# Last feed-forward of a transformer block: one activation per rounding, wider places for the output projections, x added by TensorE for half the tiles

## The chip, the cores and the metric

The kernel runs on 1 core of one Trainium2 chip. The metric is the device time of the whole program in microseconds (us). The core has five engines that matter here, each with its own in-order queue: PE (TensorE: matmuls, and transposes as matmuls with an identity), DVE (VectorE), ACT (ScalarE), POOL (GpSimd) and SP, which here issues the DMAs. They wait for one another through semaphores.

## The reference, cut to what matters

x has 2 sequences of 2048 tokens with 256 features. The block is: layer norm, attention with 16 heads, residual, layer norm, a gated feed-forward of width 704 whose operands are rounded to 4-bit floats in blocks of 16, residual.

```python
def fp4_quant_dequant(x):
    shape = x.shape
    xb = x.reshape(shape[:-1] + (shape[-1] // BLOCK, BLOCK))
    scale = jnp.max(jnp.abs(xb), axis=-1, keepdims=True) / 6.0
    scale = jnp.maximum(scale, jnp.float32(1e-12))
    xn = xb / scale
    idx = jnp.searchsorted(_MID, jnp.abs(xn))
    q = _GRID[idx] * jnp.sign(xn) * scale
    return q.reshape(shape)

def _L0_ffn_ref(x, w_gate, w_up, w_down):
    gate = fp4_linear(x, w_gate)
    y = fp4_linear(x, w_up)
    h = jax.nn.silu(gate) * y
    return fp4_linear(h, w_down)

h = _layernorm(x, axis=-1) * (1 + ca) + sa
x = x + ga * _L0_attn_ref(h, ...)
h = _layernorm(x, axis=-1) * (1 + cb) + sb
x = x + gb * _L0_ffn_ref(h, ...)
```

`fp4_linear` rounds both operands and multiplies them. sa to gb are vectors of 256 for each sequence.

## The kernel before, in words

A sequence is cut into 16 tiles of 128 tokens. The two sequences run one after the other through attention, head by head; the feed-forward of the first sequence is spread under the attention of the second. The feed-forward of the second has nothing to lie under: it is the last stage, from about 1797 us to the end, and the change touches this stage alone.

No order is written out by hand. Each piece of work is a Python generator (a chain) that yields operations. A planner, `Order`, takes the chains with a due time each, keeps an estimated clock for every engine, and emits the operation that can start earliest by its own cost estimates, preferring the chain due first within a small patience. What it emits is the order in each engine's queue. `Best` lets it choose between two engines, with a margin by which the second has to be better. Places in PSUM are handed out by name: three places "s" of two banks each, and two places "o" of one bank. `Wait` takes a place, `give` returns it. All operations are recorded by one helper, so nearly all of them carry line 253 in the profile, and tiles are told apart by their names.

In the last stage, with b = 1 and q = 3 (the last group of heads):

- `project_last` multiplies the attention output of a tile (`osb`) by the output weights (`wo`, two products of 256 columns into `op`) and adds the result to the tile of `x` on DVE. Tiles 0 and 1 have an "s" place each, of which one bank is used; then two tiles share one bank, those of 6 and 7 in an "s" place and the others in "o" places.
- `ffn_stats` computes the layer norm's statistics (`stf`, `mvf`, `ln0f` to `ln2f`) for tile 0, tiles 1 to 3, and then four tiles at a time.
- `tail_norm` applies them into `w` (one tile for 0 and 1, then two tiles of 256 side by side, 512 wide) and rounds `w` with `quantize`.
- `tail` transposes a rounded tile (`hq`, in an "o" place), copies it to SBUF, multiplies by the gate and up weights (`pg`, `pu`, an "s" place each, four products of 352 columns each), applies silu on ACT, multiplies on DVE into `e` (704 wide), rounds `e` with `quantize`, transposes it (`h2t`, an "s" place), copies it, and multiplies by the down weights `wdb` into `dn`, on top of a product of the identity with `x` that carries the residual. `tail_out` copies `dn` to `y` and stores it. For the last tile `tail_part` does this in two halves of 352.
- `quantize(a, nb, name, m, margin)` rounds in place: maximum of each block (`am`), reciprocal and scale (`r`, `s`, `q`), multiplication by `r`, the exponents of the result into `m` by a bit mask, from these a magic constant for each element, addition and subtraction of it (which rounds), and multiplication by `s`. In the last stage `margin` is a number, elsewhere it is None. For the constants the planner chooses between two passes on ACT and one on DVE. In the last stage DVE does the addition, POOL or DVE the subtraction and the last multiplication.

The due times of the last stage are relative to d, the end of the attention steps:

```python
add(
    project_last(b, NQUAD - 1, t, 1 if t < 2 else 2),
    d + PROJECT_DUE[t // 4] + (0.1 * t if t < 4 else 0.0),
)
```

Of the kernel before, what the change touches and what calls it, by code (L numbers as in the profile page):

```python
# [10 lines left out]
F32 = mybir.dt.float32  # L11
# [3 lines left out]
AF = mybir.ActivationFunctionType  # L15
ALU = mybir.AluOpType
# [4 lines left out]
P = 128  # L21
# [18 lines left out]
QUANTIZE_MARGIN = 2  # L40
WEIGHTS_MARGIN = 3
TAIL_MARGIN = 0.5
MAGIC_MARGIN = 2.0


PROJECT_DUE = -0.5, 0.0, 0.2, 0.4
NORM_DUE = -0.4, -0.2, 0.6
STATS_LEAD = 4
NORM_LEAD = 3.5
# [50 lines left out]
class Order:  # L100
# [17 lines left out]
    def add(self, gen, due, pace=0.0):  # L118

        heapq.heappush(self.later, (due, next(self.seq), gen, pace))  # L120


    def signal(self, key, of=1, early=0.0):

        n, t = self.counts.get(key, (0, 0.0))
        n, t = n + 1, max(t, self.chain.end - early)
        self.counts[key] = (n, t)
        if n == of:
            self.done[key] = t
        return n == of  # L130

    def give(self, name, n=1, place=0):
        for _ in range(n):
            heapq.heappush(self.rooms[name], (self.chain.end, place))
# [180 lines left out]
def adaln_block(  # L315
# [15 lines left out]
    B, N, D = x_in.shape  # L331
# [10 lines left out]
    NQUAD = H // 4  # L342
# [12 lines left out]
    T, V, A, G, S = (  # L355
        Queue(n, e)
        for n, e in (
            ("PE", nc.tensor),
            ("DVE", nc.vector),
            ("ACT", nc.scalar),  # L360
            ("POOL", nc.gpsimd),
            ("SP", nc.sync),
        )
# [9 lines left out]
    signal, give, due = order.signal, order.give, order.due  # L373
# [14 lines left out]
    def banks(place, name):  # L388

        return ps_s.tile([P, 2, 512], F32, tag=f"s{place}", name=name)  # L390
# [7 lines left out]
    def either(first, second, margin):  # L398
        return Best(first, second, margin=COPY_MARGIN if margin is None else margin)

    def copy(dst, src, margin=None):
        return either(A.copy(dst, src), V.tensor_copy(dst, src), margin)

    def matmuls(dst, pairs, first=True):
        return [
            T.matmul(dst, lhsT=l, rhs=r, start=(first and k == 0), stop=(k == len(pairs) - 1))
            for k, (l, r) in enumerate(pairs)
        ]
# [22 lines left out]
    def x_tile(b, t):  # L431
        return xs[b, t // 4][:, t % 4, :]
# [153 lines left out]
    def pool(*args, margin):  # L586
        if margin is None:
            return V.tensor_tensor(*args)
        return Best(G.tensor_tensor(*args), V.tensor_tensor(*args), margin=margin)
# [9 lines left out]
    SIXTH = 1.0 / 6.0  # L599

    EXPONENT = 0x7F800000

    SMALLEST = 5.999999976025183e-12

# [3 lines left out]
    def spread(s):  # L608
        return s[:, :].unsqueeze(2).to_broadcast([s.shape[0], s.shape[1], BLK])
# [17 lines left out]
    def quantize(a, nb, name, m, margin=None):  # L627

        a3 = blocks(a)
        yield Wait(take=["qs"])
        am = small.tile([P, nb], F32, tag="am", name=f"am_{name}", bufs=3)
        s = small.tile([P, nb], F32, tag="qs", name=f"s_{name}", bufs=3)
        r = small.tile([P, nb], F32, tag="qr", name=f"r_{name}", bufs=3)
        q = small.tile([P, nb], F32, tag="qq", name=f"q_{name}", bufs=2)  # L640
        yield V.tensor_reduce(am, a3, AX.X, ALU.max, apply_absolute_value=True)
        yield V.tensor_scalar(am, am, SMALLEST, None, ALU.max)
        yield V.reciprocal(r, am)

        yield Free(V.tensor_scalar(s, am, SIXTH, None, ALU.mult))
        yield V.tensor_scalar(r, r, 6.0 - 3 * 2.0 ** -21, None, ALU.mult)
        yield V.scalar_tensor_tensor(q, s, -4.0, am, ALU.mult, ALU.add)
        yield pool(a3, a3, spread(r), ALU.mult, margin=QUANTIZE_MARGIN if margin is None else None)
        yield Free(V.scalar_tensor_tensor(q, s, -2.0, q, ALU.mult, ALU.add))
        yield V.tensor_scalar(m.bitcast(U32), a.bitcast(U32), EXPONENT, None, ALU.bitwise_and)  # L650
        yield Free(V.scalar_tensor_tensor(s, q, SIXTH, s, ALU.mult, ALU.add))
        yield either(

            [
                A.activation(m, m, AF.Relu, bias=magic[:, 1:2], scale=1.5 * 2.0 ** 22),
                A.activation(m, m, AF.Identity, bias=magic[:, 0:1]),
            ],
            V.tensor_scalar(m, m, 1.0, 1.5 * 2.0 ** 22, ALU.max, ALU.mult),
            margin if margin is None else MAGIC_MARGIN,
        )  # L660
        yield pool(a, a, m, ALU.add, margin=QUANTIZE_MARGIN if margin is None else None)
        for args in ((a, a, m, ALU.subtract), (a3, a3, spread(s), ALU.mult)):
            op = G.tensor_tensor(*args)
            yield op if margin is None else Best(op, V.tensor_tensor(*args), margin=margin)
        give("qs")

    def quantize_exactly(x, i, u, name):
# [470 lines left out]
    def project_last(b, q, t, n):  # L1138

        g = t // 4  # L1140
        room = "s" if t in (0, 1, 6) else "o"
        (place,) = yield Wait(
            [("osb", b, q, g), ("wo", b, q), ("x", b, g)]
            + [("out", b, q - 1, t + j) for j in range(n)],
            [room],
        )
        name = f"op{b}_{q}_{t}"
        if room == "s":
            ps = banks(place, name)[:, 0, :]
        else:  # L1150
            ps = ps_o.tile([P, 512], F32, tag="o", name=name)
        for j in range(n):
            yield Free(
                matmuls(
                    ps[:, j * D : (j + 1) * D],
                    [
                        (o_sb[b, 2 * q + k][:, (t + j) * P : (t + j + 1) * P], wos[b, q][:, k, :])
                        for k in range(2)
                    ],
                )  # L1160
            )
        x2 = xs[b, g][:, t % 4 : t % 4 + n, :]
        yield V.tensor_tensor(x2, ps[:, 0 : n * D].rearrange("p (j d) -> p j d", d=D), x2, ALU.add)
        give(room, place=place)
        for j in range(n):
            signal(("out", b, q, t + j))

# [98 lines left out]
    def silu_table():  # L1266
        yield Wait([("w", len(steps) - 1, 0)])
        yield A.activation(sig[:, :, 0], sig[:, :, 0], AF.Silu)
# [185 lines left out]
    for b in range(B):  # L1454
        s0 = b * PER
        if b > 0:
            spread_over([norm(b, g) for g in range(NG)], s0 - 62, s0 - 36, NPACE)
            spread_over([qk(b, 0, i, n) for n in range(NCH) for i in range(2)], s0 - 36, s0 - 14)
            spread_over([qk(b, 1, i, n) for n in range(NCH) for i in range(2)], s0 + 16, s0 + 6 * NT)
            spread_over([load_x(b, g) for g in range(NG)], s0 + 2 * NT, s0 + 3 * NT)  # L1460
        for q in range(NQUAD):
            e0 = s0 + 4 * q * NT
            if (b, q) != (0, 0):
                add(load_wv(b, q), e0 - 2 * NT)
                spread_over([values(b, q, g) for g in range(NG)], e0 - NT + 3, e0 + 3)
            add(load_wo(b, q), e0 + 2 * NT)
            if (b, q) == (B - 1, NQUAD - 1):
                continue
            o0 = e0 + 4 * NT + 2
            spread_over(  # L1470
                [project(b, q, g) for g in range(NG)], o0, o0 + (20 if q == NQUAD - 1 else 40)
            )
        if b < B - 1:
            f0 = s0 + PER + 10
            for t in range(NT):
                if t % 4 == 0:
                    add(ffn_stats(b, t, 4), f0 + FFN * t - 1)
                add(ffn(b, t), f0 + FFN * t, FPACE)
        else:
            d = s0 + PER + LAG - 1  # L1480
            add(weight_tail(), s0 + PER - 6)
            add(silu_table(), d - 0.2)
            for t in (0, 1, *range(2, NT, 2)):
                add(
                    project_last(b, NQUAD - 1, t, 1 if t < 2 else 2),
                    d + PROJECT_DUE[t // 4] + (0.1 * t if t < 4 else 0.0),
                )
                if t < 4:
                    dues = d + NORM_DUE[(t + 1) // 2]
                else:  # L1490
                    dues = d + t - STATS_LEAD
                if t == lns_of(t):
                    add(ffn_stats(b, t, (1, 3)[t] if t < 4 else 4), dues)
                add(tail_norm(b, t, 1 if t < 2 else 2), dues if t < 4 else d + t - NORM_LEAD)
            for t in range(NT):
                add(tail(b, t), d + t - (LAST_LEAD if t >= NT - SPLIT else 0))
# [48 lines left out]
```

## Time and profile before

| what | us |
|---|---|
| median of 3 runs | 1987.07 |
| lowest, highest | 1986.43, 1989.49 |
| profiled execution | 1986.46 |
| its span, first to last instruction | 1984.7 |
| PE busy in the span | 1919.7 (97%) |
| DVE busy | 1714.8 (86%) |
| ACT busy | 1341.3 (68%) |
| POOL busy | 622.0 (31%) |
| granted clock of PE, mean | 0.996 |

The page gives busy time, not the bound: a matmul's end is modelled, and a queue that waits for a semaphore is not busy. In the last stage several engines hand each other tiles in turn. Between 1860 and 1880 us, for instance, PE is busy 18.75 of 20 us and DVE 19.32. By form, the last stage's rounding has these rows on ACT and DVE:

| row | count | mean ns |
|---|---|---|
| ACT, constants, 128x704 | 30 | 882 |
| ACT, constants, 128x512 | 14 | 721 |
| DVE, addition or subtraction of them, 128x704 | 29 | 900 |
| DVE, the same, 128x512 | 14 | 675 |
| DVE, multiplication by s, 128x704 | 12 | 879 |
| DVE, x plus projection, 128x512 | 7 | 686 |
| DVE, copy of `h2t`, 118x768 | 2 | 956 |

In a timeline row the first number is the start, the second the time from the first start to the last end of the merged instructions, and the bracket at the end the idle time of the engine before them and what ended it. Every fp32 product is two matmul instructions, which is why four products are listed as x8.

### The profile page before, as it was taken

To read this page: it belongs to the slowest core of one execution; us is meant where nothing else is said; L and a number is where in the kernel's file an instruction comes from. 1 tells how busy PE (TensorE), PEld (TensorE's weight loads), DVE (VectorE), ACT (ScalarE), POOL (GpSimd) and SP (SyncE) were. 2 spreads that over 40 slices of the span, in tenths; PEclk is the share of its full clock that TensorE was granted. 3 is DMA by queue.
4 is the path that set the end of the run, shared out by engine and by line. 5 is a ranking of instruction groups with operands and counts; after the bars stand their busy time and mean duration, and the time that the engine had idled before them with its cause. 6 is when DMAs were issued, how large, how long until landed. Compare 5 with 4: busy or idle time off the path is not lost. (4 is left out here: it accounts for less than half of the span.)

```text
span 1984.7 us, 30266 instructions
## 1 busy us (share of the span) xinstructions
PE 1919.7 (97%) x10196; PEld 782.1 (39%) x10196; DVE 1714.8 (86%) x4125; ACT 1341.3 (68%) x1438; POOL 622.0 (31%) x1387
## 2 busy tenths in 40 slices
PE   8999999999999989999999999999999999998988
PEld 5323333233333333343333444334343333325666
DVE  5999889988999998879888688897788878998897
ACT  3677767777777676776777667685676767783444
POOL 0233333333343331112444344444443111230100
PEclk9999999999999999999999999999999999999999
DMA  6322121112111123211011201211011111100000
GB/s 212 84 61 59 37 59 49 38 33 49 33 45 33 38 64 91 75 38 49 14 46 56 63 24 38 54 36 38 4 36 43 33 33 33 33 1 0 13 12 19
DMA packets 40395, 88.02 MB, mean 44 GB/s; under 512 B 6320, under 2 KB 22576, under 8 KB 36272
## 3 DMA queue, kind: packets, MB, share of 16 engines
q1 hardware_dynamic: 38880, 83.98, 16.4%
q10 hardware_dynamic: 1360, 2.10, 0.3%
q8 instruction: 82, 1.34, 0.3%
q14 instruction: 73, 0.60, 0.1%
HBM read 63.51 MB, written 20.97 MB: 43 GB/s over the span
## 5 line engine op out<-in xcount | busy, mean ns | idle before, releaser
L253 DVE TENSOR_SCALAR_CACHE_REDUCE e<-ps 128x1024 f32<-128x1024 f32 x1024 | 1221.7, 1218 | 141.1 <-PE ps L253 92.3
L253 ACT ACTIVATE e<-e,mn 128x2048 f32<-128x2048 f32 x512 | 1025.4, 2003 | 435.2 <-POOL mn L253 432.2
L253 PE MATMUL o<-e,vn 128*64 128x512 f32 x4096 | 995.5, 604 | 24.3 <-POOL vn L253 18.8
L253 PEld LDWEIGHTS o<-e,vn 128*64 128x64 f32 x4096 | 253.4, 136 | 482.8 <-issue 350.9
L253 POOL TENSOR_SCALAR mn<-mn 128x1 f32<-128x1 f32 x512 | 154.6, 302 | 832.9 <-DVE rz L253 344.4
L253 PE MATMUL ps<-q,k 64*128 64x512 f32 x2048 | 383.5, 448 | 5.4 <-DVE e L253 2.1
L253 PEld LDWEIGHTS ps<-q,k 64*128 64x128 f32 x2048 | 157.3, 185 | 377.9 <-DVE rz L253 109.2
L253 POOL TENSOR_SCALAR vn<-v,rz 128x64 f32<-128x64 f32 x512 | 169.4, 331 | 305.9 <-DVE rz L253 233.4
L253 PE MATMUL op<-wo,osb 128*64 128x256 f32 (+1 forms) x960 | 123.6, 382 | 2.8 <-DVE x L253 2.1
L253 PE MATMUL v<-wv,ht 128*64 128x256 f32 x1024 | 123.3, 383 | 0.6 <-DVE st L253 0.6
L253 DVE RECIPROCAL rz<-z 128x1 f32<-128x1 f32 x512 | 80.3, 157 | 27.0 <-ACT e L253 25.8
L253 PEld LDWEIGHTS op<-wo,osb 128*64 128x64 f32 (+1 forms) x960 | 76.4, 140 | 60.4 <-issue 30.7
L253 ACT ACTIVATION_READ_ACCUMULATOR e<-e,mn 128x1 f32 x512 | 95.4, 186 | 0.0
L253 PEld LDWEIGHTS v<-wv,ht 128*64 128x64 f32 x1024 | 70.5, 137 | 58.6 <-issue 25.6
L253 DVE DVE_READ_ACCUMULATOR e<-ps 128x1 f32 x1024 | 84.7, 83 | 0.0
L253 ACT COPY osb<-o 64x512 f32<-64x512 f32 x101 | 58.4, 579 | 18.6 <-PE o L253 17.2
L253 PE MATMUL qk<-ht,wqk_sb 128*64 128x512 f32 (+1 forms) x224 | 65.8, 605 | 1.3 <-ACT ht L253 0.9
L253 POOL TENSOR_TENSOR h<-h,m 128x704 f32<-128x704 f32 x32 | 54.1, 1690 | 10.3 <-DVE m L253 5.6
L253 DVE TENSOR_TENSOR x<-op,x 128x1024 f32<-128x1024 f32 (+2 forms) x37 | 39.7, 1074 | 15.9 <-PE op L253 15.6
L253 PE MATMUL pg<-wg_t,w 128*128 128x352 f32 x128 | 46.7, 507 | 6.4 <-ACT w L253 6.4
L253 PE MATMUL dn<-wdb,e 117*128 117x256 f32 (+1 forms) x192 | 45.3, 384 | 3.3 <-ACT e L253 2.5
L253 ACT ACT_TABLE_LOAD x34 | 43.6, 1283 | 4.3 <-issue 3.7
(242 smaller groups left out, 1468.8 us busy)
## 6 DMA issues: line engine op xcount, KB each, us to landing
k<-scr SPq DMA_DIRECT2D x124, 256.0 KB, 4.7
scr<-st SPq DMA_DIRECT2D x32, 512.0 KB, 3.1
q<-scr SPq DMA_DIRECT2D x124, 128.0 KB, 5.6
x<-in_x_dram SPq DMA_DIRECT2D x8, 512.0 KB, 4.9
wv<-in_wv_dram SPq DMA_DIRECT2D x8, 256.0 KB, 5.4
wo<-in_wo_dram SPq DMA_DIRECT2D x8, 256.0 KB, 4.2
xt<-in_x_dram SPq DMA_DIRECT2D x4, 512.0 KB, 5.4
out_dram<-h2t SPq DMA_DIRECT2D x16, 128.0 KB, 1.7
```

Source lines behind the costliest of these rows:

```text
L253: op = Op(self.name, *self.estimate(method, args, kw, lambda: f(*args, **kw)))
```

## The change

It has two parts, both in the last stage.

Rounding, where `margin` is a number: ACT makes the constant without its offset in one pass, Relu(MAGIC * m - MAGIC). DVE adds the offset while it adds the constant, and again while it takes the sum away, in two operations with three inputs (tile, number, tile). The second leaves the value negated, and the scale s is negated to match. The subtraction stays on DVE; the last multiplication may still go to POOL. If the planner chooses DVE for the constants, that is two operations now.

Projections: tiles 0 to 3, 4 to 7 and 8 to 11 share one "s" place of two banks each; 12 and 13, and 14 and 15, an "o" place. The additions to `x` are their own chains, `projected`: two of one tile and then of two tiles. For tiles 8 to 15 (`ADD_X = 2` groups of four and above) PE adds x by a product with the identity, and the sum is copied to `x` by ACT or DVE, whichever the planner finds better.

```diff
 PROJECT_DUE = -0.5, 0.0, 0.2, 0.4
+PROJECTED = (0, 4), (4, 4), (8, 4), (12, 2), (14, 2)
+ADD_X = 2
...
+    MAGIC = 1.5 * 2.0 ** 22
...
         yield V.tensor_scalar(m.bitcast(U32), a.bitcast(U32), EXPONENT, None, ALU.bitwise_and)
-        yield Free(V.scalar_tensor_tensor(s, q, SIXTH, s, ALU.mult, ALU.add))
-        yield either(
-
-            [
-                A.activation(m, m, AF.Relu, bias=magic[:, 1:2], scale=1.5 * 2.0 ** 22),
-                A.activation(m, m, AF.Identity, bias=magic[:, 0:1]),
-            ],
-            V.tensor_scalar(m, m, 1.0, 1.5 * 2.0 ** 22, ALU.max, ALU.mult),
-            margin if margin is None else MAGIC_MARGIN,
-        )
-        yield pool(a, a, m, ALU.add, margin=QUANTIZE_MARGIN if margin is None else None)
-        for args in ((a, a, m, ALU.subtract), (a3, a3, spread(s), ALU.mult)):
-            op = G.tensor_tensor(*args)
-            yield op if margin is None else Best(op, V.tensor_tensor(*args), margin=margin)
+        if margin is None:
...
+        else:
+
+            yield Free(V.scalar_tensor_tensor(s, q, -SIXTH, s, ALU.mult, ALU.subtract))
+            yield either(
+                A.activation(m, m, AF.Relu, bias=magic[:, 1:2], scale=MAGIC),
+                [
+                    V.tensor_scalar(m, m, 1.0, MAGIC, ALU.max, ALU.mult),
+                    V.tensor_scalar(m, m, -MAGIC, None, ALU.add),
+                ],
+                MAGIC_MARGIN,
+            )
+            yield V.scalar_tensor_tensor(a, m, MAGIC, a, ALU.add, ALU.add)
+            yield V.scalar_tensor_tensor(a, m, MAGIC, a, ALU.add, ALU.subtract)
+            op = G.tensor_tensor(a3, a3, spread(s), ALU.mult)
+            yield Best(op, V.tensor_tensor(a3, a3, spread(s), ALU.mult), margin=margin)
         give("qs")
...
-        room = "s" if t in (0, 1, 6) else "o"
+        room = "s" if n > 2 else "o"
...
         if room == "s":
-            ps = banks(place, name)[:, 0, :]
+            ps = banks(place, name)
         else:
-            ps = ps_o.tile([P, 512], F32, tag="o", name=name)
...
-        x2 = xs[b, g][:, t % 4 : t % 4 + n, :]
-        yield V.tensor_tensor(x2, ps[:, 0 : n * D].rearrange("p (j d) -> p j d", d=D), x2, ALU.add)
-        give(room, place=place)
+            ps = ps_o.tile([P, 512], F32, tag="o", name=name).unsqueeze(1)
+        taken = [1, 1, 2] if t == 0 else [2] * (n // 2)
+        for k, m in enumerate(taken):
+            first = sum(taken[:k])
+            part = ps[:, first // 2, first % 2 * D : (first % 2 + m) * D]
+            for j in range(m):
+                u = t + first + j
+                pairs = [
+                    (o_sb[b, 2 * q + c][:, u * P : (u + 1) * P], wos[b, q][:, c, :])
+                    for c in range(2)
+                ]
+                if g >= ADD_X:
+                    pairs = [(ident, x_tile(b, u))] + pairs
+                yield Free(matmuls(part[:, j * D : (j + 1) * D], pairs))
+            order.add(
+                projected(b, q, t + first, m, part, order.chain.end, (room, place, t, len(taken))),
+                order.chain.due,
+            )
+
+    def projected(b, q, t, n, ps, ready, where):
+
+        room, place, first, parts = where
+        order.chain.base = ready + order.CROSS
+        x2 = xs[b, t // 4][:, t % 4 : t % 4 + n, :]
+        ps = ps.rearrange("p (j d) -> p j d", d=D)
+        if t // 4 >= ADD_X:
+            yield copy(x2, ps, TAIL_MARGIN)
+        else:
+            yield V.tensor_tensor(x2, ps, x2, ALU.add)
+        if signal(("projected", b, q, first), of=parts):
+            give(room, place=place)
         for j in range(n):
             signal(("out", b, q, t + j))
...
             add(silu_table(), d - 0.2)
+            for t, n in PROJECTED:
+                add(project_last(b, NQUAD - 1, t, n), d + PROJECT_DUE[t // 4])
             for t in (0, 1, *range(2, NT, 2)):
-                add(
-                    project_last(b, NQUAD - 1, t, 1 if t < 2 else 2),
-                    d + PROJECT_DUE[t // 4] + (0.1 * t if t < 4 else 0.0),
-                )
                 if t < 4:
```

## The prediction, made before the changed kernel had run

> **What bounds the kernel now.** I read the windows first, then TensorE's timeline over the last stage, then DVE's waits, then the rows by form. Attention up to 1796 us is untouched: the changed program issues the same instructions in the same order on every engine there. So everything is decided in the last feed-forward, 1797 to 1984.7 us. The windows (busy us of PE, PEld, DVE, ACT, POOL, then granted clock, DMA):
>
> ```profile
> core 0: us, PE busy (x) PEld busy (x) DVE busy (x) ACT busy (x) POOL busy (x), PEclk, DMA share, GB/s
> 1800.00:1820.00 20.00, 12.26 (x50) 9.30 (x49) 19.80 (x98) 2.81 (x7) 0.00 (x0) 0.87 0.00 0
> ...
> 1840.00:1860.00 20.00, 17.63 (x71) 12.38 (x70) 15.59 (x44) 7.88 (x12) 1.38 (x2) 0.91 0.02 7
> ...
> 1880.00:1900.00 20.00, 19.30 (x79) 13.74 (x78) 18.11 (x58) 9.32 (x15) 1.07 (x1) 1.00 0.06 20
> 1900.00:1920.00 20.00, 18.52 (x79) 13.14 (x79) 19.52 (x55) 9.36 (x15) 1.06 (x1) 1.00 0.04 14
> 1920.00:1940.00 20.00, 16.44 (x71) 12.03 (x70) 17.75 (x49) 8.83 (x15) 1.64 (x1) 0.91 0.04 14
> ```
>
> First DVE is full and PE waits; later both are nearly full, and ACT is never half busy. Where PE waits (start, us, form, count, then the wait before it):
>
> ```profile
> 1796.98 10.63 PE L253 MATMUL op<-wo,osb 128*128 128x256 f32 x48
> 1809.70 1.99 PE L253 MATMUL op<-wo,osb 128*128 128x256 f32 x8 [2.09 <-DVE x L253]
> 1816.88 0.69 PE L253 MATMUL hq<-ident,w 128*128 128x128 f32 x2 [5.19 <-DVE x L253]
> 1818.03 4.40 PE L253 MATMUL pg<-wg_t,w 128*128 128x352 f32 x8 [0.46 <-ACT w L253]
> 1822.27 2.53 PE L253 MATMUL pu<-wu_t,w 128*128 128x352 f32 x8
> 1824.64 1.89 PE L253 MATMUL op<-wo,osb 128*128 128x256 f32 x8
> ...
> 1848.77 4.33 PE L253 MATMUL pg<-wg_t,w 128*128 128x352 f32 x8 [1.51 <-ACT w L253]
> ...
> 1869.68 2.63 PE L253 MATMUL pg<-wg_t,w 128*128 128x352 f32 x8 [0.79 <-ACT w L253]
> ...
> 1928.63 0.84 PE L253 MATMUL h2t<-ident,e 128*118 128x128 f32 x6 [3.04 <-DVE e L253]
> ...
> 1950.92 1.45 PE L253 MATMUL pg<-wg_t,w 128*128 128x352 f32 x4 [1.05 <-ACT w L253]
> ```
>
> The first transposes (`hq_0`) wait for DVE's `x` addition and not for the normed tile: w_0 was finished at 1811.0, but both "o" places still held projections. After that wait, and again at 1848.77, the gate product takes 4.4 instead of 2.6: granted clock 0.87 and 0.91. DVE has one long wait of its own, because a copy of transposed data stands in its queue:
>
> ```profile
> 1856.16 0.96 DVE L253 COPY e<-h2t 118x768 f32<-118x768 f32 x1 [3.54 <-PE h2t L253]
> ```
>
> **The change, step by step.** Starts are read from the timeline; pitches are differences of starts: 0.2165 us per matmul instruction of 256 columns (two to a product), so 0.87 for a tile's projection; gate or up product 2.37; DVE 0.34/0.60/0.80 for two-input work 256/512/704 wide.
>
> *Start.* Tiles 8 to 15 get one product each for x: 8 x 0.43 = 3.5 us more PE. In the changed program's queues the waits go by whole places: the addition of tile 0 waits for tile 1's product, tile 2's product for that addition, tile 3's for the next, tile 7's for the addition of 4 and 5, tile 11's for ACT's copy of 8 and 9. From 1797.05: tile 1 ends 1798.8, the first addition starts 1799.0 (now 1798.15), tiles 2, 3, 7 and 11 are held 0.7, 0.6, 0.85 and 0.85 us. PE: 16 x 0.87 + 3.5 + 3.0 held + 0.2 for hq_0 = 20.6, so pg_0 starts about 1817.7 (now 1818.03). DVE reaches w_0 at 1813.4, which is 2.4 later than now: additions start 0.9 later and then wait for products (1.7 more), one w_1 operation of 0.4 moves ahead, and one addition of 0.6 is gone. That is covered: hq_0 stands behind tile 14 and starts at 1816.2. Without the cover it would cost those 2.4.
>
> *Clock and last projection.* PE's longest idle is now 0.9, so pg_0 runs at 2.37 rather than 4.24 to the next start (1.87), and the two projections after pu_0 (1.73) are already done. hq_1 starts 1822.4 against 1826.37: 0.3 + 1.9 + 1.7 = 4.0 gained. DVE has w_1 ready by 1820.7, having four additions fewer; ACT's four copies of 512 (nearest row: 0.586, a 512-wide PSUM copy) lie in its idle time, but the last of them, released at 1817.7, is ahead of w_1's constants; that holds DVE about 0.3.
>
> *Rounding.* ACT loses one pass per quantization: 0.88 at 704 (15 times), 0.72 at 512 (7), about 0.5 at 256 and 352 (4). DVE's two plain additions become two three-input ones. No 704-wide row of these without pointer exists. The nearest: qx_wd 128x352 at 517 ns against 517 for a plain one, qx_wg 128x256 at 418 against 412; so no cost. Upper end: those with pointers at 256, 476 against 410, 0.055 x 52 (two in each of 26 roundings) = 2.9 us. Lower end 0. POOL takes four multiplications by s_g instead of three and a subtraction, no change; SP's queue is identical. All DVE pitches summed: 158.1 us now, 153.5 after: four additions (2.4) and three copies go to ACT (2.2).
>
> *Tiles 0 to 5.* DVE's times here are the pitches summed in the changed order from 1799.0, plus its waits: 1.8 for products, 0.9 where small dependent operations start 0.19 apart and nothing fills in, 0.3 for ACT, then 0.6 for pu_0, together 3.6; PE's are its products in a row. hq_2 needs w_2 from POOL, ready 1827 before pu_1 ends at 1827.9; h2t_0, free at 1837.1, has its e_0 and the place it takes at 1835.8. dn_0 ends 1842.0 (now 1846.2). Then w_4: DVE 1799.0 + 38.8 + 3.6 = 1841.4, POOL 1.06 to 1.64 behind it, so hq_4 at 1843.0 and, one ACT pass less in its queue, pg_4 at 1843.9: a gap of 1.9 for 2.6 now. With the clock kept (1.8), pu_4 ends at 1848.6 against 1855.3: 4.2 + 0.7 + 1.8 = 6.7. Such gaps, from the last product to the next with transposes between, were 2.3 before 1950.92, warm (x4 in 1.45), and 2.6 before 1848.77, cold. 1.9 is below both, so I take warm; cold costs 1.8. The Trainium skill, "TensorE: Matmul & The Clock Gate" (What's actually happening), says the clock falls after an idle window of about 3.4 us, and Part 4 there that transposes do not count as busy. By the window 1.9 stays warm, the trace's 2.6 should have too and did not; by Part 4 the total could fall to 6.7 us.
>
> *Onward.* COPY e_1 goes to ACT and its 3.54 wait with it; h2t_1 comes 6.7 earlier. dn_1, dn_2 hold 0.5 each for ACT copies; pg_6 starts 1862.6 (now 1869.68): 7.1. DVE ends w_6's rounding at 1799.0 + 54.4 + 3.6 = 1857.0 (now 1865.05), so it isn't what PE waits for at hq_6. From there work is alike on both (DVE 99.1 after, 99.4 now; same PE work), so I keep the gap. Added: the wait at 1928.63, whose chain runs through ACT pairs, shortens by one pass, 0.9; the last tile loses a pass of 0.5 on the chain that ends last. Sum: 7.1 + 0.9 + 0.5 = 8.5.
>
> The Trainium skill, "PSUM — Partial Sum Buffer" (PSUM bank collisions raise a hardware error), forbids two engines only in one bank at once; by it tile 2, in the second bank, need not wait, which would give about 0.7 back. The program waits by place, so the trace should show the holds.
>
> The profiled execution took 1986.46, span 1984.7; the median of the three unprofiled runs is 1987.07, 0.6 above, and I carry that over: 1987.07 - 8.5 = **1978.6 us**.
>
> **Rivals.** (A) *More*: the 3.04 wait at 1928 and its cold restart (pg x4 2.52 for 1.35, and slow dn, together 1.9) go entirely: 4.0 on top, 1974.6. For: ACT's queue there holds two pairs, 1.80 and 1.48, halved. Against: two tiles cost DVE about 18.9 of the present 19.1 cadence, so lateness may reappear elsewhere. 0.17.
> (B) *Given back*: DVE is the bound; only its removed work counts, less its later start: 4.6 - 2.4 = 2.2, 1984.9. For: 19.52 of 20 busy in 1900 to 1920. Against: 15.59 in 1840 to 1860, which is PE's lateness. 0.15.
> (C) *Slower*: ACT becomes DVE's gate. Constants and copies share one in-order queue; each copy that waits for PE holds a rounding behind it, and DVE's queue with it. DVE now waits 4.0 us for this in 26 roundings (3.6 and 0.4 by the rows of e), 0.15 each; were each as long as the single wait of 0.64 at 1869, it is 26 x 0.49 = 12.7 more, 1991.3. It decides from 8.5/26 = 0.33 more each. Against: ACT 9.4 of 20 busy, and a pass fewer. 0.08.
> That the change does nothing is excluded: in the queues each constants pass stands once, x is copied by ACT.
>
> **Numbers.** Forecast 0.60, A 0.17, B 0.15, C 0.08. A measurement of this kernel tells about 0.2% (4 us) from no change: faster 0.60 + 0.17 = 0.77, same 0.15, slower 0.08. Range: A and another 1.1 down, 1973.5; up the cold pg_4 (1.8), dearer rounding (2.9) and the unshortened wait (0.9), with 0.3 towards B: 1984.5.
>
> **What would show it.** hq_0 at 1816 with no wait on `x`; pg_0 at 2.4 to 2.6; four short holds among the projections; pg_4 near 1844 and warm; no h2t copy on DVE; three-input rounding rows at 0.88. I am wrong if PE falls to the low clock among the projections, if DVE's waits for ACT exceed 12 us, or if pg_6 is early and the end is not.

## The result, and the profile after

The changed kernel took 1976.99 us (median of 4 runs, 1974.49 to 1977.45) against 1987.43 for the kernel before (4 runs): a ratio of 0.9944, 95% interval 0.9926 to 0.9961. So it is faster by 10.4 us.

The profiled execution of the changed kernel has a span of 1975.7 against 1984.7, 9.0 less. But it entered the last stage late: attention's last product ended at 1799.34 us, and at 1797.05 in the execution of before. The instructions up to there are the same, but TensorE's granted clock was 0.50 for three stretches of 3.41 us in this execution (from 22, 49 and 616 us) and for one in that of before (from 47 us). Over the fourteen profiled executions of this study the stage is entered between 1796.1 and 1799.8. Every edit here touches only what comes after it, so from here on kernels are compared by their **stage**: from the end of attention's last product to the end of the span. It was 187.65 us before and is 176.36 now: 11.3 less. (The expectations below count from the first projection product: 0.07 earlier, but in runs 4 and 12 0.44 later, because there it waits for ACT.)

The windows of the changed kernel, with the columns as before (busy us of PE, PEld, DVE, ACT, POOL, then the granted clock, DMA):

```profile
core 0: us, PE busy (x) PEld busy (x) DVE busy (x) ACT busy (x) POOL busy (x), PEclk, DMA share, GB/s
1800.00:1820.00 20.00, 17.51 (x79) 14.12 (x78) 16.54 (x82) 5.04 (x9) 0.00 (x0) 1.00 0.00 0
...
1840.00:1860.00 20.00, 18.15 (x84) 13.45 (x83) 19.79 (x56) 7.22 (x12) 1.21 (x1) 1.00 0.04 13
...
1920.00:1940.00 20.00, 17.76 (x75) 12.41 (x74) 19.42 (x49) 7.41 (x12) 3.80 (x3) 1.00 0.06 20
```

The clock is 1.00 in all three, where before it was 0.87, 0.91 and 0.91. DVE, which had 15.59 of 20 us to do in 1840 to 1860, is nearly full there.

TensorE's timeline of the changed kernel, at the places shown of before (start, us, form, count, and the wait before it):

```profile
1801.78 1.13 PE L255 MATMUL op<-wo,osb 128*128 128x256 f32 x4 [0.52 <-DVE x L255]
1803.43 3.72 PE L255 MATMUL op<-wo,osb 128*128 128x256 f32 x16 [0.52 <-DVE x L255]
1807.93 1.13 PE L255 MATMUL op<-wo,osb 128*128 128x256 f32 x4 [0.78 <-DVE x L255]
...
1813.62 0.70 PE L255 MATMUL op<-x,ident 128*128 128x256 f32 x2 [0.68 <-ACT x L255]
...
1818.91 0.38 PE L255 MATMUL hq<-ident,w 128*128 128x128 f32 x2
...
1820.42 2.53 PE L255 MATMUL pg<-wg_t,w 128*128 128x352 f32 x8
...
1846.70 2.63 PE L255 MATMUL pg<-wg_t,w 128*128 128x352 f32 x8 [0.44 <-ACT w L255]
...
1866.08 2.63 PE L255 MATMUL pg<-wg_t,w 128*128 128x352 f32 x8 [0.29 <-ACT w L255]
...
1925.95 0.66 PE L255 MATMUL hq<-ident,w 128*128 128x128 f32 x4 [0.94 <-POOL w L255]
1926.90 2.63 PE L255 MATMUL pg<-wg_t,w 128*128 128x352 f32 x8 [0.30 <-ACT w L255]
```

The four holds among the projections are there, the wait of 5.19 for `x` is gone, and no gate product runs at the low clock. The longest wait in the whole stage is the 0.94 near 1926, for POOL; near 1928 before had one of 3.04, for DVE.

The stage can be taken apart on TensorE: products at full clock, with the 3.2 us that follow the last of them, plus idle time, plus what the low clock adds. Idle time is the sum of the waits in the timeline. The changed kernel has hardly a slow product, and 176.36 - 11.50 idle = 164.86; without the eight products with x (0.433 each) it is 161.4. What another kernel has beyond that is put down to the clock (runs 4 and 8 below, whose clock did not fall before the last product, come out at -0.2 and 0.5, which shows how exact this is):

| kernel | stage | idle of PE | clock | median of runs |
|---|---|---|---|---|
| before | 187.65 | 20.7 | 5.6 | 1987.43 |
| changed | 176.36 | 11.5 | 0 | 1976.99 |

So 9.2 us of idle time and 5.6 of slow clock went, and 3.5 of products came in.

By form, DVE's two three-input operations and ACT's one pass (count, then busy us and mean ns of one, then the idle time before):

```profile
L255 DVE SCALAR_TENSOR_TENSOR e<-e 128x704 f32<-128x704 f32 x30 | 26.4, 880 | 1.9 <-ACT e L255 1.9
...
L255 ACT ACTIVATE e<-e,magic 128x704 f32<-128x704 f32 x15 | 13.2, 881 | 8.6 <-DVE e L255 8.6
```

880 ns against 900 for the plain additions and subtractions before, and at 512 wide 686 against 675: the third input costs nothing to speak of.

### The profile page after: what moved, and what is told of

It is laid out like the page before. It is cut to its first block, busy times and chain, and to the rows that moved or that the text cites. A ratio compares the mean times of both kernels' runs of the same rounds, so it can differ in the third digit from the quotient of the medians.

```text
span 1975.7 us, 30282 instructions
## 1 busy us (share of the span) xinstructions
PE 1920.0 (97%) x10212; PEld 783.1 (40%) x10212; DVE 1711.3 (87%) x4118; ACT 1325.7 (67%) x1419; POOL 621.0 (31%) x1387
## 5 line engine op out<-in xcount | busy, mean ns | idle before, releaser
L255 DVE RECIPROCAL rz<-z 128x1 f32<-128x1 f32 x512 | 80.4, 157 | 27.0 <-ACT e L255 25.8
L255 ACT COPY osb<-o 64x512 f32<-64x512 f32 x101 | 58.4, 579 | 18.6 <-PE o L255 17.2
L255 PE MATMUL dn<-wd_t,h2t 117*64 117x256 f32 (+1 forms) x384 | 46.2, 383 | 0.2 <-DVE h2t L255 0.2
```

The source lines that it names most:

```text
L255: op = Op(self.name, *self.estimate(method, args, kw, lambda: f(*args, **kw)))
```

## The experiments

Twelve kernels, all with the same attention. The table has their stage, TensorE's idle time and the clock's share as above, and the median of the whole runs. The kernel before, run beside them, had medians of 1987.43, 1988.42 and 1987.24 in the three groups (1 to 4, 5 to 8, 9 to 12).

| run | stage | idle | clock | median | ratio to before, 95% interval |
|---|---|---|---|---|---|
| 1 rounding only | 176.79 | 13.8 | 1.6 | 1976.95 | 0.9951, 0.9934 to 0.9968 |
| 2 projections only | 188.26 | 18.8 | 4.6 | 1987.13 | 0.9999, 0.9990 to 1.0009 |
| 3 x added on DVE | 187.90 | 22.1 | 4.4 | 1987.53 | 1.0004, 0.9994 to 1.0013 |
| 4 first tiles apart | 175.56 | 10.9 | -0.2 | 1975.49 | 0.9944, 0.9929 to 0.9959 |
| 5 two passes | 179.51 | 12.3 | 2.4 | 1978.68 | 0.9955, 0.9940 to 0.9970 |
| 6 two passes, unplanned | 184.67 | 15.9 | 3.9 | 1984.93 | 0.9980, 0.9971 to 0.9990 |
| 7 one pass, planned two | 178.55 | 11.4 | 2.3 | 1978.12 | 0.9953, 0.9938 to 0.9968 |
| 8 scale on POOL | 175.56 | 10.2 | 0.5 | 1974.60 | 0.9935, 0.9919 to 0.9952 |
| 9 two passes, old order | 187.91 | 18.6 | 4.4 | 1987.28 | 1.0001, 0.9992 to 1.0010 |
| 10 one pass, old order | 188.03 | 18.0 | 5.2 | 1987.93 | 1.0005, 0.9996 to 1.0014 |
| 11 before's order, one pass | 182.32 | 18.8 | 2.1 | 1983.46 | 0.9984, 0.9975 to 0.9993 |
| 12 apart and POOL | 174.76 | 9.6 | 0.3 | 1975.17 | 0.9940, 0.9926 to 0.9953 |

A stage is that of one execution, and the clock's share differs from one execution of a kernel to the next: the ten of run 6 took 1979.35 us (mean clock 1.000) to 1986.05 (0.996). The medians bear out the large steps below: runs 7 and 10 are 9.8 apart, run 6 is 7.9 above the changed kernel, run 11 is 3.8 below before. Differences of about 1 us in the stage they don't tell.

### The two parts by themselves (runs 1 and 2)

Run 1 takes the new `quantize` and leaves `project_last` as it was; run 2 the other way round.

> The new rounding with the old projections. The measure is the length of the last stage, from its first projection product to the end of the span: 187.7 us before, 176.4 after. Theory 1 (the prediction's steps: TensorE's waits and its clock set the stage): the start is as before, hq_0 waits 5 us for x and pg_0 runs cold at 4.4, so nothing is gained by hq_1; later one ACT pass less is worth 0.7 at pg_4, perhaps 1.8 of clock there, 0.9 at the wait of 3.04, 0.5 at the end: a gain of 2 to 4, stage 184 to 186. Theory 2 (DVE's full queue sets the stage, and what counts is its work plus the waits that ACT's second pass put into it): DVE has two multiplications and three copies fewer than before, 3.8, and loses its waits for the copies of h2t, 5.0: a gain of 8 to 9, stage about 179.

> The new projections with the old rounding (two ACT passes, two-input additions). Stage 187.7 before, 176.4 after. Theory 1: the start gains 4.0 by hq_1 and the clock at pg_4 1.8 more, the later waits stay: a gain of 5 to 7, stage 181 to 183, with pg_0 at 2.4 to 2.6. Theory 2: DVE saves four additions and adds a copy of y, one less h2t copy than now is not saved: its work falls by about 1.4, and its waits for ACT stay: a gain of 1 to 3, stage 185 to 187.

Rounding alone does nearly everything: 176.79, a gain of 10.9 of the 11.3. The new projections alone gain nothing: 188.26. Theory 1 is refuted on both. Theory 2 is nearer, and still 2 us off for run 1 and 1.3 beyond its range for run 2: it counted DVE's work and waits, and not what else a new order moves.

In run 1, with the old projections, the first transposes are not as late as before. At the start TensorE's queue has the same order there, but DVE's has not. An addition to `x` frees the place that `hq_0` takes. In the kernel before it stands behind the first steps of `w_1`:

```profile
1816.14 0.68 DVE L253 TENSOR_TENSOR x<-op,x 128x512 f32<-128x512 f32 x1
```

In run 1 it stands ahead of them (and TensorE's timeline after it: start, us, form, wait):

```profile
1811.56 0.68 DVE L253 TENSOR_TENSOR x<-op,x 128x512 f32<-128x512 f32 x1
...
1812.29 0.44 PE L253 MATMUL hq<-ident,w 128*128 128x128 f32 x2
1813.23 2.63 PE L253 MATMUL pg<-wg_t,w 128*128 128x352 f32 x8 [0.51 <-ACT w L253]
...
1843.44 0.70 PE L253 MATMUL hq<-ident,w 128*128 128x128 f32 x4 [2.26 <-POOL w L253]
1844.38 4.08 PE L253 MATMUL pg<-wg_t,w 128*128 128x352 f32 x8 [0.24 <-ACT w L253]
```

Attention ended at 1797.61 here, so the addition starts at 13.95 in the stage instead of 19.09, and `hq_0` at 14.7, 5.1 earlier than before (19.8), without a wait. With one pass less to count, the planner had put down another order on DVE.

In run 2 the start gains most of what was predicted, and gives it back:

```profile
1847.50 0.66 PE L255 MATMUL hq<-ident,w 128*128 128x128 f32 x4 [3.94 <-POOL w L255]
...
1889.60 1.51 PE L255 MATMUL h2t<-ident,e 128*118 128x128 f32 x6 [3.67 <-DVE e L255]
```

`hq_1` is at 25.8 in the stage, as in the changed kernel and 3.5 earlier than before. But `hq_4` then waits 3.94 for tile `w_4` and stands at 50.6; before it stood at 49.1, and in the changed kernel at 46.3. Being early at the start is worth nothing when the next tile isn't.

### The product with x, and the holds (runs 3 and 4)

```diff
-ADD_X = 2
+ADD_X = 4
```

> The changed kernel without the products with x: all sixteen tiles of x are added on DVE, places and rounding as in the changed kernel. TensorE does 3.5 us less among the projections, ACT four copies less, DVE four additions more (2.4) and two multiplications more that the planner takes back from POOL (1.6). Theory 1: pg_0 starts 1 to 2 us earlier and the end follows, stage 174.5 to 176. Theory 2: DVE's 4.0 more come out at the end, stage 179 to 180.5.

The stage was 187.90, worse than either expected. One line of TensorE's timeline shows most of it:

```profile
1825.49 0.69 PE L255 MATMUL hq<-ident,w 128*128 128x128 f32 x2 [9.07 <-DVE x L255]
1826.70 4.87 PE L255 MATMUL pg<-wg_t,w 128*128 128x352 f32 x8 [0.52 <-ACT w L255]
```

In the new places both "o" places hold projections until DVE has added them, and DVE's queue comes to those additions late: 9.07 us of wait, then a cold gate product of 4.87. The products with x buy ACT's copies in place of them. They go with the new places: run 1 has neither and is as fast. Whether the new places could do without them in another order wasn't tried; this edit, too, made the planner put down a new one.

Run 4 gives the first tiles places of their own and leaves the order on every engine as it is:

```diff
-PROJECTED = (0, 4), (4, 4), (8, 4), (12, 2), (14, 2)
+PROJECTED = (0, 1), (1, 1), (2, 2), (4, 4), (8, 4), (12, 2), (14, 2)
...
-        room = "s" if n > 2 else "o"
+        room = "s" if n > 2 or t == 2 else "o"
...
-        taken = [1, 1, 2] if t == 0 else [2] * (n // 2)
+        taken = [1] if n == 1 else [2] * (n // 2)
```

> The changed kernel with tiles 0 and 1 in an o place of their own and tiles 2 and 3 in an s place, so that the first additions and products no longer wait for one another's place; the work and the order of every engine from the first normed tile on are the same. The traced holds of 0.52 and 0.52 before tiles 2 and 3 go, and DVE's first addition starts some 0.8 earlier. If holds among the projections reach the end: pg_0 and the end 0.8 to 1.1 earlier, stage 175.3 to 175.6. If they are covered by later waits: pg_0 earlier, the end within 0.3 of 176.4.

The two holds of 0.52 went, `pg_0` started 0.7 earlier in the stage (20.35 against 21.08), `hq_12` 0.7, the end 0.8. With the order fixed, what is won at the start does reach the end.

### The pass or the order (runs 5 to 7)

Two things changed when the second ACT pass went: the pass itself, and the order that the planner puts down when it counts one pass. These runs cross the two. `again` is an identity on the constants; all else is the changed kernel.

```diff
+            first = A.activation(m, m, AF.Relu, bias=magic[:, 1:2], scale=MAGIC)
+            again = A.activation(m, m, AF.Identity, scale=1.0)
             yield either(
-                A.activation(m, m, AF.Relu, bias=magic[:, 1:2], scale=MAGIC),
+                [first, again],
```

That is run 5. Run 6 emits `again` with `first` but leaves `first.cost`; run 7 adds `again.cost` to `first.cost` and doesn't emit it.

> The changed kernel with a second ACT pass behind each constants pass (an identity, which alters no value), and the planner is told. So ACT again makes two passes for each of 26 roundings while DVE's form stays new. Stage 176.4 in the changed kernel, 187.7 before, 188.3 with the old rounding in the new places. If the pass is the cause (by its length in the chain or by what the planner makes of it): stage 185 to 189. If the form on DVE is the cause (three-input operations, negated scale): stage 176 to 179.

> The same second ACT pass, but the planner counts one only: every engine keeps exactly the order of the changed kernel, and ACT has 26 passes more, about 20 us of its idle time. Theory P (the pass's own length, because DVE's next operations in its queue are the additions that wait for it): DVE's waits for ACT grow by 0.3 to 0.5 for each of 26 roundings, stage 184 to 190. Theory Q (the planner's order: it moved copies to DVE and placed work differently when it counted two passes; ACT has room): stage 176.5 to 179.

> One ACT pass as in the changed kernel, but the planner counts the cost of two: the order of the kernel with two passes, run with one. DVE gets one copy of h2t (0.87) and one of y (0.34) more. Theory P: the order matters little, stage 176.5 to 179. Theory Q: stage 184 to 188.

Run 5 came out at 179.51, just beyond the range of the "form" side; but see runs 9 and 10. Run 6 came out at 184.67, so theory P holds in that order: DVE's queue has the addition right behind, and waits. Its waits for ACT in the stage sum to 13.5 us, against 5.6 in the changed kernel; the two longest:

```profile
1854.21 0.89 DVE L255 SCALAR_TENSOR_TENSOR e<-e 128x704 f32<-128x704 f32 x1 [2.26 <-ACT e L255]
...
1895.76 0.89 DVE L255 SCALAR_TENSOR_TENSOR e<-e 128x704 f32<-128x704 f32 x1 [2.42 <-ACT e L255]
```

Run 7 at 178.55 is inside theory P's range. In the order made for two passes, the second costs only 1.0 (179.51 against 178.55); in the order made for one it costs 8.3. The price of a pass depends on the order that it is put in.

### The same order with either form and either number of passes (runs 9 to 11)

Run 5 left 8.7 us open: it has two passes and the new places, as run 2 has, and is that much shorter. Two things still differed: DVE's form, and 0.093 us in the planner's cost of the second pass (the old one had a bias). Run 9 is run 5 with that 0.093 added:

```diff
             again = A.activation(m, m, AF.Identity, scale=1.0)
+            again.cost += 0.093
```

> As the kernel of two passes with the planner told, but the second pass is counted 0.093 us dearer, as the old pass with its bias was. That makes the planner put down the order of the run with only the new projections (TensorE's and ACT's queues word for word, DVE's and POOL's up to the subtraction of w_10, which there went to POOL). Only DVE's form differs from that run: three inputs, negated. Stage lengths so far: 179.6 with two passes, 188.3 with only the new projections. If the order is what costs the 8.7: stage 186 to 189. If the old form on DVE is: stage 178 to 181.

Run 10 is run 7 with 0.093 added, so the same order with one pass.

> The same order again (the planner counts two passes, the second with its bias), run with one pass. If the order costs most and the pass little, as between the first pair (178.6 with one pass, 179.6 with two): stage 185 to 188. If the passes make the waits that this order suffers from: stage 177 to 181.

187.91 and 188.03. So the order alone costs 8.4 of the 8.7; the old form on DVE costs nothing that shows (188.26 in run 2 against 187.91), and in this order even the second pass costs nothing. Runs 7 and 10 execute the same work, but for one multiplication that moves from POOL to DVE and two copies of `h2t` that move from ACT to DVE, and are 9.5 us apart: 6.6 of TensorE's idle time and 2.9 of its clock.

Where the two part can be seen at tile `w_4`. First run 10: the second of DVE's two rounding operations on `w_4`, POOL's multiplication, then TensorE:

```profile
1847.57 0.69 DVE L255 SCALAR_TENSOR_TENSOR w<-w 128x512 f32<-128x512 f32 x1
1848.40 1.57 POOL L255 TENSOR_TENSOR w<-w,s_h 128x512 f32<-128x512 f32 x1 [18.18 <-DVE w L255]
1850.02 1.12 PE L255 MATMUL hq<-ident,w 128*128 128x128 f32 x4 [3.94 <-POOL w L255]
1851.22 4.45 PE L255 MATMUL pg<-wg_t,w 128*128 128x352 f32 x8
```

And run 7, the same steps, with one of POOL's more ahead of them:

```profile
1837.18 1.39 POOL L255 TENSOR_TENSOR e<-e,s_g 128x704 f32<-128x704 f32 x1 [7.41 <-DVE e L255]
...
1843.84 0.69 DVE L255 SCALAR_TENSOR_TENSOR w<-w 128x512 f32<-128x512 f32 x1
1844.67 1.21 POOL L255 TENSOR_TENSOR w<-w,s_h 128x512 f32<-128x512 f32 x1 [6.11 <-DVE w L255]
1845.93 0.66 PE L255 MATMUL hq<-ident,w 128*128 128x128 f32 x4 [0.72 <-POOL w L255]
```

Attention ended at 1799.47 and 1799.35. In run 7 POOL takes the multiplication of `e_0` and DVE goes on; in run 10 DVE does it itself (0.74 to the next start), copies a `y` (0.34), and has other tiles' steps ahead of `w_4`. So `w_4`'s second rounding operation starts at 48.1 in the stage instead of 44.5, TensorE waits 3.94 instead of 0.72, and that wait costs it the clock: the gate product behind it takes 4.45. Run 2 has this wait to the hundredth.

Run 11 is the cross in the old places: before's order, one pass.

```diff
+            first.cost += again.cost + 0.093
```

> The old projections and the order of the kernel before on every engine (up to the subtraction of e_13, near the end, which was on POOL and is on DVE), but each rounding with one ACT pass and DVE's new form. Stage 187.7 before, 176.9 with the old projections and the new rounding in the planner's own order. If the planner's order, not the pass itself, is most of the gain: stage 184 to 187. If the pass itself is: stage 177 to 180.

182.32, below the one range and above the other. So of run 1's 10.9 us, 5.3 come with before's order kept (near the end the subtraction of `e_13` went from POOL to DVE with it, and a multiplication and half a copy moved too) and 5.5 from the planner's new order. Of the 5.3, 1.9 is idle time and 3.5 the clock; by the medians, the 5.3 is 3.8, so the split is good to some 1.5 us. TensorE's gate products at the two places where they were cold before:

```profile
1850.54 2.63 PE L253 MATMUL pg<-wg_t,w 128*128 128x352 f32 x8 [0.61 <-ACT w L253]
...
1927.44 0.84 PE L253 MATMUL h2t<-ident,e 128*118 128x128 f32 x6 [2.13 <-DVE e L253]
...
1929.49 1.45 PE L253 MATMUL pg<-wg_t,w 128*128 128x352 f32 x4 [0.57 <-ACT w L253]
```

2.63 instead of 4.33, and 1.45 instead of 2.52, though the waits before them only became 0.9 us shorter each: the pass is gone from both.

### Taking work off DVE (runs 8 and 12)

```diff
+LAST_MARGIN = 1.0
...
-            yield Best(op, V.tensor_tensor(a3, a3, spread(s), ALU.mult), margin=margin)
+            yield Best(op, V.tensor_tensor(a3, a3, spread(s), ALU.mult), margin=LAST_MARGIN if margin else 0.0)
```

> The changed kernel with the last multiplication of every rounding from tile 1 on POOL (the margin by which DVE must be better is 1.0, not 0.5): 11 multiplications of 0.80 leave DVE, 8.8 us, and POOL does each in 1.39 with a hand-over more. If DVE's queue sets the stage: 4 to 8 us less, stage 168.5 to 172.5 of 176.4, and PE's idle time of 11.5 falls. If PE's chain of waits sets it (theory 1): each hidden tile arrives 0.7 later and nothing is gained, stage 176 to 180.

175.56: 0.8 less, neither range. DVE's busy time in the stage fell from 157.6 to 153.2, 4.4 and not 8.8. Some rows became longer, such as this one, 308 ns against 237 (run 8, by form):

```profile
L256 DVE SCALAR_TENSOR_TENSOR s_g<-q_g,s_g 128x44 f32<-128x44 f32 x15 | 4.6, 308 | 0.0
```

The mean hides that thirteen of the fifteen kept their 0.19 to 0.27 us. One of the other two took 0.59, and one 1.39, until POOL's multiplication was over:

```profile
1942.57 1.51 POOL L256 TENSOR_TENSOR e<-e,s_g 128x704 f32<-128x704 f32 x1 [5.87 <-DVE e L256]
...
1942.75 1.39 DVE L256 SCALAR_TENSOR_TENSOR s_g<-q_g,s_g 128x44 f32<-128x44 f32 x1
```

And DVE's own waits grew by 3.3 (14.8 to 18.1): those for products in `e` from 2.8 to 8.4, while those for ACT fell. So DVE's work alone isn't the bound; what counts, as runs 7 and 10 show, is when each tile's steps come up in its queue.

Run 12 has runs 4 and 8 in one.

> The changed kernel with both gainful edits: first tiles in places of their own, last multiplications on POOL. Alone they had medians of 1975.5 and 1974.6 against 1977.0. If the two add: median 1973 to 1973.5, stage about 174.8 by the same count. If DVE's or PE's next wait takes it back: no better than the better one alone, 1974.6 to 1976.

The stage is 174.76, as expected if the two add, 1.6 below the changed kernel's. The median of the whole runs, 1975.17, doesn't show it: it lies in the range for a gain taken back, and the intervals of runs 4, 8 and 12 all overlap that of the changed kernel. So run 12 beats the changed kernel in the stage, but not by what the whole time can tell.

## Why the prediction was right in time and wrong in its cause

**The time.** Forecast 1978.6 and a gain of 8.5; measured 1976.99 and 10.4. In the stage it was 11.3.

**The start** came as worked out. From the end of attention, the first addition was due at 1.95 and came at 1.96; the holds were forecast as 0.7, 0.6, 0.85 and 0.85 and were 0.52, 0.52, 0.78 and 0.68. `pg_0` was due at 20.65 and came at 21.08, so that its own gain of 0.3 was none (20.98 before). It was warm, and `hq_1` gained 3.5 of the 4.0.

**Rounding.** The three-input form at no cost (880 ns; the other 704-wide rows of two inputs have 868 to 881) and the 0.3 us of DVE's wait for ACT at `w_1` (0.30) were right.

**Tiles 0 to 5.** `hq_4` was due at 45.95 and came at 46.27, `pg_4` at 46.85 and came at 47.36, and warm: after a gap of 1.50 us between products, where 1.9 was forecast (from the end of a product as the timeline shows it, the forecast's gaps of 2.3 and 2.6 are 2.14 and 2.42). The gain at the end of `pu_4` was 6.1 for 6.7. The rule of the Trainium skill, "TensorE: Matmul & The Clock Gate" (Part 4), that transposes do not count as busy the same way, lowered nothing at a gap of this length.

**Onward.** The two holds of `dn` for ACT were 0.51 and 0.50 for 0.5. `pg_6` gained 5.9, not 7.1. But then the stage gained 5.4 more, and the forecast had 1.4: the wait of 3.04 and its cold restart did not shorten by 0.9, they vanished. That is rival A's event. From `pg_6` on, TensorE's idle time fell by 3.5 net, although three waits for POOL came in (0.87, 0.39 and 0.94), and the clock gave 1.9. The two errors have opposite signs, 1.2 too much and 4.0 too little.

**The step that failed** is the one that gave the gain to the parts of the change. The sum puts 4.0 and most of the 6.7 down to the start, that is to the projections, and to the missing pass 0.7 at `pg_4`, 0.9 and 0.5, some 2 in all. The runs say the reverse: projections alone -0.6, rounding alone 10.9. The positions were read from the changed program's queues, and those were already shaped by the planner's counting one pass instead of two. So the time came out near, and the reason didn't: the step that carries the 4.0 of `hq_1` on as 4.2 at `dn_0` and `w_4` holds only in a queue order in which `w_4` is early too, and that order came from what the planner counted for the rounding, not from the projections. Run 2 has the lead and loses it in one wait of 3.94. That the time fitted is in part luck: the two errors partly cancelled, and run 10 shows nearly the same work back at the time of before, by the planner's order alone.

**The rivals.** A's event happened, within a stage gain between the forecast and A's 12.5, but A's reason, ACT's halved pairs, is not enough for it: in run 11, with before's order and one pass, the wait is still 2.13, shorter by the 0.9 of the forecast. The rest came with the order. B, that DVE's removed work alone counts, would have given 2.2; and run 8, which takes 4.4 more off DVE for 0.8, speaks against it as a rule. C was wrong: DVE's waits for ACT are 5.6 us in the stage (1.1 for `w`, 4.5 for `e`), far from the 12 named, but more than the 4.0 before, although a pass is gone. Run 6 shows that its mechanism is real: with a second pass in this order these waits are 13.5 and the stage is 8.3 longer.

**What stays open.** The order that run 10 shares with run 2 has three more long waits for DVE (3.25, 1.48 and 1.27 before `h2t` in run 10). They were not followed through DVE's queue as the one at `w_4` was.

## What to carry to other kernels

Where a planner decides the order, the diff of a cost is a diff of the whole order: 0.093 us in the estimate of one ACT pass moved the end by 9.5 us with nearly the same work. To find what an edit earns, cross the two: run the new work in the old order, and the old work in the new one. And a stage-by-stage forecast that meets the time hasn't shown which edit earned it: one run of each part by itself shows that, and the crossed runs whether it is the work or the order.

## What the runs showed of the hardware

**The clock of TensorE** doesn't follow the length of a gap alone. In the fourteen traces, between the end of a product and the start of the next (transposes in between not counted), every gap up to 2.27 us was followed by gate products at full clock (2.63 us for eight), and every one from 4.84 up by slow ones (4.2 to 4.9 for eight, 2.1 to 2.7 for four). Between the two both happened: slow after, among others, 2.32 (4.33), 2.42 (4.33), 2.92 (4.12) and 3.20 (4.08), full after 2.34 (2.63), 2.70 (2.63), 3.48 (1.45 for four) and 4.18 (1.45).

The granted clock in the traces shows why. In the last stage it fell to 0.50 for 3.41 us, or for two or three times that (6.83, 10.24), and within one execution the falls are whole multiples of 3.41 us apart (1814.82, 1848.95 and 1930.87 in the kernel before). So in these traces it falls only at points that lie a fixed step apart, elsewhere in each execution, and what counts is the 3.41 us ahead of such a point. In those ahead of 1848.95 in the kernel before, products filled 1.0 us and transposes 0.7, and the clock fell. In those from 1926.59 in run 11, products filled 0.5 and transposes 1.5, and it stayed up; so here transposes count for something. The Trainium skill, "TensorE: Matmul & The Clock Gate" (What's actually happening), has a free-running idle window of about 3.4 us. Length and free running agree with the trace; that the window has to be idle doesn't, and there the measurement decides. A gap of two us between products was safe here; one of 2.3 to 4.2 was a matter of where it lay.

**POOL beside DVE.** Eleven multiplications moved from DVE to POOL took 4.4 us off DVE's busy time instead of 8.8. In the fourteen last stages, every operation of DVE that took over 60 ns more than the median of its form overlapped an instruction of POOL; what they took more sums to 6.3 us in run 8 and to 2.7 in the changed kernel. The Trainium skill, "SBUF — State Buffer" (Who interferes with whom), says that an operation of DVE with two inputs in SBUF contends with one of POOL that reads SBUF; the two lines of run 8 above agree, where DVE's operation ends 0.06 us after POOL's. An operation with one input was held as well: `am_g` at 1894.38 in run 8 took 1.07 us instead of 0.18, beside a multiplication of POOL from 1894.35 to 1895.41.
